# Attention, router and experts on one core: three banks for scores, four for maxima, another order within a step, and a lead-in in program order

## The chip, the core and the metric

The kernel runs on one core of one Trainium2 chip. A core has TensorE (PE, matrix products; its weight loads are shown as PEld), VectorE (DVE), ScalarE (ACT), GpSimd (POOL) and SyncE (SP), which here only issues DMAs. Matmuls write into PSUM, which has eight banks of 128 partitions x 512 float32; DVE and ACT read it. The metric is device time in microseconds (us) of one execution, lower is better. The time before is the median of three runs, 2309.47 us (2308.5 to 2316.39).

## The reference

One block of attention, a small mixing layer and a mixture of experts over x of shape 2 x 2048 x 256, all in float32:

```
qkv = x @ qkv_w + qkv_b                    # 16 heads of 16
q, k = rot(q), rot(k)                      # angles depend on the head, not on the place
attn = softmax(q @ k^T / 4)
x = layernorm(x + (attn @ v) @ out_w + out_b)
n = layer_norm(x, g1, be1)
y = x + n + (n @ mix_w + mix_b)
n = layer_norm(y, g2, be2)
probs = softmax(n @ router_w); the best 2 of 8 experts, with their weights
out = sum over the 2 of  weight * (silu(n @ w1[e] + b1[e]) @ w2[e] + b2[e])
x = layernorm(x + y + out)
```

The scores, 2 x 16 x 2048 x 2048 of them, are the bulk of the work: each is computed twice on PE, once to find the maximum of its row and once to be exponentiated.

## The kernel before

**Visits and steps.** A visit is one batch, one block of 512 queries and one group of four heads: 2 x 4 x 4 = 32 visits. A visit has 16 steps, one for each block of 128 keys, so that the attention loop has 512 steps. In a step:

- `scores(w, kt, pair)`, for two pairs of heads: two matmuls of keys by queries (L503) into two PSUM tiles, then two matmuls (L512) that add each query's negated maximum, then two exponentials on ACT (L518), each 128x512, that read those tiles. The two matmuls of a pair use different halves of PE's rows and run side by side.
- `values(w, kt, exs)`: four products of the exponentials with the values (L533), into the accumulator `av`, for the step before.
- `maxima(t, half)`, twice: two matmuls of queries by keys (L459) into two PSUM tiles, and two reductions by DVE (L467) that keep each row's maximum. They run `AHEAD` = 19 steps ahead of the scores, since a visit's maxima have to be complete before its first score.
- `work(1.0)`: small work that falls due, from a list ordered by step: transposes and projections of the next x (`prep_x`, `prep_qk`, `prep_v`), division and turning of a finished visit, the projection, the normalisations, the mixing layer, the router, and the lists of tokens per expert.

The order of PE, ACT, DVE and SP is written by hand (`manual_schedule`): each does its instructions in the program's order and waits where a semaphore is not there yet. POOL is ordered by the framework. Before, a step stands in this order: scores of both pairs, first half of the maxima, values of the step before, small work, second half of the maxima.

**Banks.** `ps_sc` has four PSUM banks for scores, `ps_mx` three for maxima and small work, `ps_av` one for the values. A pool hands its banks out in turn, so that a new tile of `ps_sc` may be written when the tile of four tiles ago has been read by ACT, and one of `ps_mx` when the tile of three tiles ago has been read. `bank(name)` gives a tile of `ps_sc` in the lead-in and of `ps_mx` afterwards; the maxima use it too.

**Lead-in.** Before the loop come the loads (x, weights, constants `cst`, tables `cs`), the rotation of the weights for q and k (L262 to L264, 24 small operations, all on DVE), the transposes of x (`prep_x`), the products for q and k (`qk_parts`) and the values. `split` in `qk_parts` divides each product into a high and a low part (L373 on DVE, L377 on DVE or POOL) and stores them four times over to memory (`stack`, L382), from where `load_stack` (L421) brings them as `km` and `qm`, the operands of maxima and scores. Then come 19 steps of maxima alone, between which `piece()` puts one matmul group of preparation after each half. Here the order was given by the framework up to the maxima.

**After the loop** the tokens, collected per expert in `x_list`, are run through the experts in 46 tiles: `turn_tile` transposes a tile's tokens (L1190, read by DVE at L1194) into a bank of its own pool `ps_t`; `hidden` and `add_tile` do the products. The last block's small work runs in between.

Of the kernel before, what the change touches and what calls it, by code (L numbers as in the profile page):

```python
# [24 lines left out]
F32 = mybir.dt.float32  # L25
# [38 lines left out]
def seq_postln_kernel(  # L64
# [86 lines left out]
    ps_mx = ctx.enter_context(tc.tile_pool(name="ps_mx", bufs=3, space=PSUM))  # L151

    with ExitStack() as actx:
# [4 lines left out]
        ps_sc = actx.enter_context(tc.tile_pool(name="ps_sc", bufs=4, space=PSUM))  # L158
# [25 lines left out]
        def load_x(b, tb):  # L184
            n = b * TPB + tb

            pool, tag, bufs = (ap_, f"km{tb % 2}", 3) if b == 0 else (ep, "x_in", 1)
            x_in[b, tb] = pool.tile([P, 4, D], F32, name=f"x_in_{n}", tag=tag, bufs=bufs)
            eng = nc.gpsimd if b == 0 and tb > 0 else nc.sync
            eng.dma_start(out=x_in[b, tb], in_=xv[n])  # L190

        with tc.tile_pool(name="wraw", bufs=1) as wp:
            wr = bp.tile([P, 2, H, 3, HD], F32, name="wr", tag="zx", bufs=1)
            cs = wp.tile([P, 2, H, 8], F32, name="cs")
            load_x(0, 0)
# [5 lines left out]
            nc.sync.dma_start(out=cst_sb, in_=cst)  # L201
            nc.scalar.dma_start(
                out=cs.rearrange("p a h d -> p (a h d)"), in_=rope.partition_broadcast(P)
            )
            for i in range(2):
                nc.gpsimd.memset(mt[i], 0.0)
            load_x(0, 1)
            load_x(0, 2)
            load_x(0, 3)
# [25 lines left out]
            dense = bp.tile([P, 4, HD], F32, name="dense", tag="comb", bufs=1)  # L235
            nc.vector.tensor_copy(dense, ident.rearrange("p (j r) -> p j r", r=32)[:, :, 0:HD])
            dense = dense.rearrange("p j d -> p (j d)")

            t3 = bp.tile([P, 2, G], F32, name="t3", tag="rest", bufs=1)
# [13 lines left out]
            for s in range(2):  # L253
                for c in range(2):
                    u1, u2 = wr[:, c, :, s, 0:8], wr[:, c, :, s, 8:16]
                    for dst, a, b_, op in (
                        (wqk[:, c, s, :, 0:8], u1, u2, ALU.subtract),
                        (wqk[:, c, s, :, 8:16], u2, u1, ALU.add),
                    ):
                        t1 = wp.tile([P, H, 8], F32, name="t1", tag="t1", bufs=2)  # L260
                        t2 = wp.tile([P, H, 8], F32, name="t2", tag="t2", bufs=2)
                        nc.vector.tensor_mul(t1, a, cs[:, 0])  # L262
                        nc.vector.tensor_mul(t2, b_, cs[:, 1])
                        nc.vector.tensor_tensor(dst, t1, t2, op)  # L264
            for c in range(2):
                nc.scalar.copy(wv[:, c], wr[:, c, :, 2, :])

            for p in range(2):
                t5 = wp.tile([P, 1], F32, name="t5", tag="t5", bufs=2)
                nc.vector.tensor_add(  # L270
                    t5, ident[:, 2 * p : 2 * p + 1], ident[:, 2 * p + 1 : 2 * p + 2]
                )
                for at in (64 + 2 * p, 65 + 2 * p):
                    nc.vector.tensor_add(t5, t5, ident[:, at : at + 1])
                nc.vector.tensor_copy(sel[p], t5.to_broadcast([P, P]))
# [17 lines left out]
        AHEAD = 19  # L293
# [37 lines left out]
        xT: dict = {}  # L331
        stack: dict = {}
# [15 lines left out]
        def qk_parts(b, tb, s, hh):  # L348


            first = leading[0]
            full, hi = (
# [18 lines left out]
            def split():  # L371

                nc.vector.tensor_single_scalar(  # L373
                    hi.bitcast(I32), full.bitcast(I32), HIGH, ALU.bitwise_and
                )
                lo = full
                (nc.vector if first and hh == 0 else nc.gpsimd).tensor_sub(lo, full, hi)  # L377
                name = f"st_{b}_{tb}_{s}_{hh}"
                t = dp.tile([8, HD, 4, 512], F32, name=name, tag=name)
                stack[b, tb, s, hh] = t  # L380
                for r, part in enumerate((hi, lo, hi, lo) if s == 0 else (hi, hi, lo, lo)):
                    (nc.sync if first else nc.gpsimd).dma_start(  # L382
                        out=t[:, :, r].rearrange("h d s -> (h d) s"), in_=part
                    )
# [33 lines left out]
        def load_stack(dst, b, tb, s, g, pair):  # L418

            at = 4 * (g % 2) + 2 * pair  # L420
            (nc.gpsimd if leading[0] else nc.sync).dma_start(  # L421
                out=dst.bitcast(F32),
                in_=stack[b, tb, s, g // 2][at : at + 2].rearrange("h d r s -> (h d r) s"),
            )

        def load_k(w):
            b, _, g = visits[w]
            km[w] = [
                ap_.tile([P, S], F32R, name=f"km_{w}_{pair}", tag=f"km{pair}", bufs=3)
                for pair in range(2)  # L430
            ]
            for tb in range(TPB):
                for pair in range(2):
                    load_stack(km[w][pair][:, tb * 512 : (tb + 1) * 512], b, tb, 1, g, pair)

        def load_q(w):
            b, qb, g = visits[w]
            qm[w] = []
            for pair in range(2):
                t = ap_.tile([P, 512], F32R, name=f"qm_{w}_{pair}", tag=f"qm{pair}", bufs=3)  # L440
                load_stack(t, b, qb, 0, g, pair)
                qm[w].append(t)

# [3 lines left out]
        def maxima(t, half):  # L447
# [8 lines left out]
            ps = [bank("ps_mx", 512) for _ in range(2)]  # L456
# [581 lines left out]
        for tb in range(TPB):  # L1038
            for c in range(2):
                prep_x(0, tb, c)  # L1040
            if tb == 0:
                dense_bias()
                prep_qk(0, 0, 0, 0)
            prep_qk(0, tb, 1, 0)
        for kt in range(0, 4, 2):
            prep_v(0, kt)
        load_q(0)
        load_k(0)
        load_q(1)
        load_k(1)  # L1050

        make_values()


        pieces: list = []
        for tb, s in [(tb, 1) for tb in range(TPB)] + [(0, 0)]:
            pieces.append(("qk", tb, s))
        for k, kt in enumerate(range(4, 16)):
            pieces.insert(1 + k + k // 2, ("v", kt))
        soon: list = []  # L1060

        def piece():

            for item in list(soon):
                item[0] -= 1
                if item[0] <= 0:
                    soon.remove(item)
                    item[1]()
            if not pieces:
                return  # L1070
            item = pieces[0]
            if item[0] == "qk":
                _, tb, s = pieces.pop(0)
                first, second, split = qk_parts(0, tb, s, 1)
                pieces.insert(0, ("fn", second, split))
                first()
            elif item[0] == "fn":
                _, second, split = pieces.pop(0)
                second()
                soon.append([2, split])  # L1080
            else:
                prep_v(0, pieces.pop(0)[1], 1)

        now[0] = 0
        at = 12
        for tb in range(1, TPB):
            small_steps(at, qk_items(0, tb, ((0, 0), (0, 1))))
            at += 4
        for tb, at in enumerate((38, 52, 104, 168)):
            later(at - 6, lambda tb=tb: load_x(1, tb))  # L1090
            small_steps(at, [(prep_x, 0.5, 1, tb, c) for c in range(2)])
            small_steps(
                at + 3,
                qk_items(1, tb, ((1, 0), (1, 1), (0, 0), (0, 1))) + v_items(1, tb),
            )
        for w in range(2, len(visits)):
            later(16 * w - AHEAD - 10, lambda w=w: load_k(w))
            later(16 * w - AHEAD - 6, lambda w=w: load_q(w))
        later(8, load_rest)
        later(36, lambda: nc.sync.dma_start(out=acc[B * S :], in_=none[:, 0:D]))  # L1100
        later(37, no_tokens)

        def max_step(t, half):
            if t < NSTEP:
                maxima(t, half)

        ET = mybir.EngineType
        with tc.manual_schedule(engines={ET.PE, ET.Activation, ET.DVE, ET.SP}):
            for t in range(AHEAD):
                now[0] = t - AHEAD  # L1110
                for half in range(2):
                    max_step(t, half)
                    piece()
                work(1.0)
            leading[0] = False
            before = None
            for t in range(NSTEP):
                now[0] = t
                w, kt = divmod(t, 16)
                exs = scores(w, kt, 0) + scores(w, kt, 1)  # L1120
                max_step(t + AHEAD, 0)
                if before is not None:
                    values(*before)
                work(1.0)
                max_step(t + AHEAD, 1)
# [8 lines left out]
    ps_t = ctx.enter_context(tc.tile_pool(name="ps_t", bufs=1, space=PSUM))  # L1134
# [49 lines left out]
    def turn_tile(t, xg):  # L1184
        ns = xg.shape[1]
        xT = wtp.tile([P, 2, ns * P], F32, name=f"xT_{t}", tag="xgT", bufs=2)
        ps = ps_t.tile([P, 2, ns * P], F32, name="ps_x", tag="t")
# [64 lines left out]
    with tc.manual_schedule(engines={ET.PE, ET.Activation, ET.DVE, ET.SP}):  # L1252
# [135 lines left out]
```

## Time and profile before

| what | value |
|---|---|
| median of three runs | 2309.47 us |
| the profiled execution's own time | 2315.68 us |
| its span in the profile | 2313.9 us |
| attention loop, from the first L503 on | from 93.1 us |
| steps of the loop that last 2.7 us, of 512 | 208 |
| L467, reductions of maxima on DVE | 2048, busy 1271.9 us, mean 682 ns |
| L518, exponentials on ACT | 2048, busy 1057.4 us, mean 604 ns |
| L459, matmuls of maxima | 2048, busy 576.0 us |
| L503 and L512, matmuls of scores | 2048 each, busy 422.6 and 419.3 us |
| L533, matmuls of values | 4096, busy 546.6 us |
| mean granted clock of TensorE | 0.985 |

The profile is one execution taken by the hardware profiler. A row of its groups names line, engine, operation, what it writes and reads, shapes and count, then busy time and the mean of one, then the engine's idle time before such instructions and what ended it. Matmuls are pipelined and their ends are modelled: the starts are recorded, and the time from one start to the next is what an instruction costs PE. The mean of an ACT or DVE instruction holds some time that overlaps the next one's start, so that busy time, a union, is less than count times mean. A weight load (PEld) goes ahead of its matmul and takes the matmul's wait: an idle time before it that ends with a reduction or an exponential may be only the time in which PE still ran earlier matmuls.

### The profile page before, as it was taken

To read this page: it belongs to the slowest core of one execution; us is meant where nothing else is said; L and a number is where in the kernel's file an instruction comes from. 1 tells how busy PE (TensorE), PEld (TensorE's weight loads), DVE (VectorE), ACT (ScalarE), POOL (GpSimd) and SP (SyncE) were. 2 spreads that over 40 slices of the span, in tenths; PEclk is the share of its full clock that TensorE was granted. 3 is DMA by queue.
4 is the path that set the end of the run, shared out by engine and by line. 5 is a ranking of instruction groups with operands and counts; after the bars stand their busy time and mean duration, and the time that the engine had idled before them with its cause. 6 is when DMAs were issued, how large, how long until landed. Compare 5 with 4: busy or idle time off the path is not lost.

```text
span 2313.9 us, 39706 instructions
## 1 busy us (share of the span) xinstructions
PE 2228.6 (96%) x14178; PEld 1337.4 (58%) x14178; DVE 1539.9 (67%) x3120; ACT 1380.4 (60%) x2722; POOL 480.4 (21%) x841
## 2 busy tenths in 40 slices
PE   6999999999999999999999999999999999999993
PEld 3445555545545555555555555555547888888882
DVE  4878778878878888888888888888815111111114
ACT  2367667766766777777777767777783222223333
POOL 3020211240123112011211201112123322222123
PEclk9799999999999999999999999999999999999996
DMA  7343321231222112112111212111046776668994
GB/s 271 114 144 119 137 101 56 74 128 62 95 99 94 46 55 74 47 66 89 66 47 56 74 49 98 56 65 56 10 132 193 207 207 192 192 187 241 305 305 155
DMA packets 173397, 275.64 MB, mean 119 GB/s; under 512 B 21648, under 2 KB 105872, under 8 KB 173200
## 3 DMA queue, kind: packets, MB, share of 16 engines
q1 hardware_dynamic: 149888, 222.95, 29.1%
q0 software_dynamic: 22896, 49.24, 7.7%
q8 instruction: 112, 1.84, 0.3%
q10 hardware_dynamic: 416, 0.92, 0.1%
q14 instruction: 85, 0.70, 0.1%
HBM read 210.31 MB, written 62.74 MB: 118 GB/s over the span
## 4 chain that ended last, share of the span: by engine, by line
PE 86%; DVE 8%; DMA 3%; issue 1%; ACT 1%; POOL 0%; SPq 0%; ACTq 0%; POOLq 0%; DVEq 0%
PE av L533 20%; PE ps_mx L459 17%; PE ps_h L1215 10%; PE ps_y L1230 10%; PE ps_sc L503 9%; PE ps_sc L512 9%; DVE pm L467 4%; PE ps_qk L361 2%; PE ps_p L594 1%; PE ps_mix L594 1%; PE ps_v L404 1%; DMA st<-full 1%; PE ps_m L491 1%; PE ps_o L555 1%; DMA b<-in_b 1%
## 5 line engine op out<-in xcount | busy, mean ns | idle before, releaser
L467 DVE TENSOR_REDUCE pm<-ps_mx 128x1 f32<-128x512 f32 x2048 | 1271.9, 682 | 201.9 <-PE ps_mx L459 197.9
L518 ACT ACTIVATE ex<-ps_sc 128x512 f32<-128x512 f32 x2048 | 1057.4, 604 | 348.9 <-PE ps_sc L512 335.9
L459 PE MATMUL ps_mx<-km,qm 64*128 64x512 f32 x2048 | 576.0, 474 | 25.9 <-DVE pm L467 17.4
L459 PEld LDWEIGHTS ps_mx<-km,qm 64*128 64x128 f32 x2048 | 289.2, 185 | 453.0 <-DVE pm L467 325.2
L533 PE MATMUL av<-ex,vt 128*32 128x512 f32 x4096 | 546.6, 605 | 0.0
L503 PE MATMUL ps_sc<-qm,km 64*128 64x512 f32 x2048 | 422.6, 395 | 0.1
L512 PE MATMUL ps_sc<-mrow,sel 64*128 64x512 f32 x2048 | 419.3, 392 | 0.0
L1222 ACT ACTIVATE hT<-ps_h,b 128x256 f32<-128x256 f32 (+1 forms) x368 | 156.2, 425 | 365.7 <-PE ps_h L1215 349.1
L1215 PE MATMUL ps_h<-xT,w 128*128 128x256 f32 (+1 forms) x1472 | 274.3, 336 | 5.1 <-ACT hT L1222 2.7
L1230 PE MATMUL ps_y<-w,hT 128*128 128x256 f32 x1136 | 255.6, 381 | 2.0 <-DVE y L1240 2.0
L1215 PEld LDWEIGHTS ps_h<-xT,w 128*128 128x128 f32 x1472 | 226.6, 190 | 48.0 <-ACT hT L1222 20.5
L1230 PEld LDWEIGHTS ps_y<-w,hT 128*128 128x128 f32 x1136 | 213.2, 191 | 29.7 <-DVE y L1240 2.4
L512 PEld LDWEIGHTS ps_sc<-mrow,sel 64*128 64x128 f32 x2048 | 204.7, 185 | 42.3
L503 PEld LDWEIGHTS ps_sc<-qm,km 64*128 64x128 f32 x2048 | 204.9, 185 | 37.9 <-ACT ex L518 14.4
L1194 DVE TENSOR_SCALAR xT<-ps_x,cols_sb 128x256 f32<-128x256 f32 (+1 forms) x92 | 40.2, 478 | 247.0 <-PE ps_x L1190 247.0
L1242 POOL DMA_INDIRECT acc<-y,xg x71 | 110.3, 1553 | 377.1 <-DVE y L1241 163.7
L533 PEld LDWEIGHTS av<-ex,vt 128*32 128x32 f32 x4096 | 81.0, 108 | 128.2 <-issue 120.5
L1240 DVE TENSOR_TENSOR y<-ps_y,b 128x256 f32<-128x256 f32 x71 | 30.1, 424 | 177.9 <-PE ps_y L1230 177.7
L132 POOL TENSOR_SCALAR op_mul<-mv 128x4 f32<-128x4 f32 x18 | 4.1, 230 | 440.7 <-DVE mv L606 439.8
L377 POOL TENSOR_TENSOR full<-full,hi 128x512 f32<-128x512 f32 x27 | 34.5, 1279 | 187.5 <-DVE hi L373 187.4
L361 PE MATMUL ps_qk<-xT,wqk 128*128 128x512 f32 x128 | 67.8, 649 | 1.1 <-ACT xT L346 1.1
L369 ACT ACTIVATE full<-ps_qk,bqk 128x512 f32<-128x512 f32 x32 | 22.0, 688 | 76.1 <-PE ps_qk L361 36.5
(201 smaller groups left out, 1149.3 us busy)
## 6 DMA issues: line engine op xcount, KB each, us to landing
w<-in_w SPq DMA_DIRECT2D x92, 1024.0 KB
km<-st SPq DMA_DIRECT2D x240, 256.0 KB
qm<-st SPq DMA_DIRECT2D x60, 256.0 KB
st<-hi POOLq DMA_DIRECT2D x44, 256.0 KB
st<-full POOLq DMA_DIRECT2D x44, 256.0 KB
xg<-x_list SPq DMA_DIRECT2D x25, 258.0 KB
b<-in_b SPq DMA_DIRECT2D x46, 128.0 KB
st<-hi SPq DMA_DIRECT2D x20, 256.0 KB
```

The source lines that it names most:

```text
L361: nc.tensor.matmul(ps, lhsT=wqk[:, c, s, 8 * hh : 8 * hh + 8, :].rearrange("p h d -> p (h d)"), rhs=xT[b, tb][:, c, :], start=(c == 0), st ...
L459: nc.tensor.matmul(ps[j], lhsT=qm[w][pair][r, qt * P : (qt + 1) * P], rhs=km[w][pair][r, kb * 512 : (kb + 1) * 512], start=True, stop=True,)
L467: nc.vector.tensor_reduce(pm[w][:, qt, 2 * pair + j, kb : kb + 1], ps[j], AX.X, ALU.max)
L503: nc.tensor.matmul(sc[j], lhsT=km[w][pair][r, kt * P : (kt + 1) * P], rhs=qm[w][pair][r, :], start=True, stop=False,)
L512: nc.tensor.matmul(sc[j], lhsT=sel[pair][r, :], rhs=mrow[w][r, :], start=False, stop=True)
L518: nc.scalar.activation(ex, sc[j], AF.Exp, scale=0.25)
L533: nc.tensor.matmul(av[32 * h : 32 * h + 32, :], lhsT=vt[b][:, kt, at : at + 32], rhs=exs[h], start=(kt == 0), stop=(kt == 15),)
L594: nc.tensor.matmul(ps[:, i, :], lhsT=turned_in[:, c, at], rhs=w[:, c, :], start=(c == 0), stop=(c == 1),)
L1215: nc.tensor.matmul(ps, lhsT=w1t[:, c, k * P : (k + 1) * P], rhs=xT[:, c, :], start=(c == 0), stop=(c == 1),)
L1222: nc.scalar.activation(hT[:, k, :], ps, AF.Silu, bias=b1[:, k : k + 1])
L1230: nc.tensor.matmul(ps, lhsT=hT[:, k, s * P : (s + 1) * P], rhs=w2t[:, k, :], start=(k == 0), stop=(k == NFC - 1),)
L1242: nc.gpsimd.indirect_dma_start(out=acc, out_offset=bass.IndirectOffsetOnAxis(ap=xg[:, s, D : D + 1].bitcast(I32), axis=0), in_=y, in_offse ...
```

## The change

It has five parts.

1. `ps_sc` gets three banks and `ps_mx` four. The maxima always take theirs from `ps_mx`, in the lead-in too.
2. A step's order becomes: scores of the first pair, values of the step before, small work, scores of the second pair, both halves of the maxima. `AHEAD` goes from 19 to 18.
3. The lead-in stands in program order on PE, ACT, DVE and SP. The constants and tables are loaded first; the other three loads of x go from POOL's queue to SP's and wait for the first operation of the rotation. The rotation for k moves to POOL, that for q stays on DVE. Four matmuls on zeros start PE. The selection columns (`make_sel`) and the copies of `wv` come later. Before the maxima begin, x of three of four blocks is prepared instead of all four; the rest goes between the halves.
4. The first products of batch 0 (`at_once`: all of k, and the first block of q, for the first eight heads) are written by DMA straight into `km` and `qm` of visit 0, 32 partitions at a time, on the queues of SP and POOL in turn; their stores to memory follow in steps 2 to 6 of the lead-in, and visit 1's loads, now on SP's queue, in step 8. Three of the six other projections of q that were small work of the first steps of the loop are done between the halves of the lead-in.
5. `ps_t` goes: `turn_tile` takes its bank from `ps_mx`.

```diff
-    ps_mx = ctx.enter_context(tc.tile_pool(name="ps_mx", bufs=3, space=PSUM))
+    ps_mx = ctx.enter_context(tc.tile_pool(name="ps_mx", bufs=4, space=PSUM))
...
-        ps_sc = actx.enter_context(tc.tile_pool(name="ps_sc", bufs=4, space=PSUM))
+        ps_sc = actx.enter_context(tc.tile_pool(name="ps_sc", bufs=3, space=PSUM))
...
-            eng = nc.gpsimd if b == 0 and tb > 0 else nc.sync
-            eng.dma_start(out=x_in[b, tb], in_=xv[n])
+            return nc.sync.dma_start(out=x_in[b, tb], in_=xv[n]).ins
...
+            rotate(nc.gpsimd, 1)
...
+            turned_ = rotate(nc.vector, 0)
+
+            for tb in range(1, TPB):
+                wait_for(load_x(0, tb), turned_[:1])
...
-        AHEAD = 19
+        AHEAD = 18
...
+            at_once = first and hh == 0 and (s == 1 or tb == 0)
...
+                for pair in range(2 if at_once else 0):
+                    to = km[0][pair][:, tb * 512 : (tb + 1) * 512] if s else qm[0][pair]
+                    to = to.bitcast(F32).rearrange("(h d r) s -> r (h d) s", d=HD, r=4)
+                    for r, part in enumerate(parts):
+                        (nc.sync, nc.gpsimd)[r % 2].dma_start(
+                            out=to[r], in_=part[32 * pair : 32 * pair + 32, :]
+                        )
...
-            ps = [bank("ps_mx", 512) for _ in range(2)]
+            ps = [ps_mx.tile([P, 512], F32, name="ps_mx", tag="mx") for _ in range(2)]
...
+            late_q = [(TPB - 2, 1), (TPB - 1, 0), (TPB - 1, 1)]
+            pieces: list = [("x", TPB - 1, c) for c in range(2)] + [("qk", TPB - 1, 1, 0)]
+            more = [("qk", tb, 1, 1) for tb in range(TPB)]
+            more += [("qk", tb, 0, hh) for tb in range(TPB) for hh in range(2) if (tb, hh) not in late_q][1:]
...
             for t in range(AHEAD):
                 now[0] = t - AHEAD
+                if t == 8:
+                    load_q(1)
+                    load_k(1)
+                elif 2 <= t < 7:
+                    stores.pop(0)()
...
-                exs = scores(w, kt, 0) + scores(w, kt, 1)
-                max_step(t + AHEAD, 0)
+                exs = scores(w, kt, 0)
                 if before is not None:
                     values(*before)
                 work(1.0)
+                exs = exs + scores(w, kt, 1)
+                max_step(t + AHEAD, 0)
                 max_step(t + AHEAD, 1)
                 before = (w, kt, exs)
...
-    ps_t = ctx.enter_context(tc.tile_pool(name="ps_t", bufs=1, space=PSUM))
...
-        ps = ps_t.tile([P, 2, ns * P], F32, name="ps_x", tag="t")
+        ps = ps_mx.tile([P, 2, ns * P], F32, name="ps_x", tag="mx")
```

## The prediction

> **What bounds the kernel now.** I read the page's busy shares and its chain of waits first, to learn which engine sets the time and in which stage.
>
> ```profile
> PE 2228.6 (96%) x14178; PEld 1337.4 (58%) x14178; DVE 1539.9 (67%) x3120; ACT 1380.4 (60%) x2722; POOL 480.4 (21%) x841
> ...
> PE 86%; DVE 8%; DMA 3%; issue 1%; ACT 1%; POOL 0%; SPq 0%; ACTq 0%; POOLq 0%; DVEq 0%
> PE av L533 20%; PE ps_mx L459 17%; PE ps_h L1215 10%; PE ps_y L1230 10%; PE ps_sc L503 9%; PE ps_sc L512 9%; DVE pm L467 4%; PE ps_qk L361 2%; PE ps_p L594 1%; PE ps_mix L594 1%; PE ps_v L404 1%; DMA st<-full 1%; PE ps_m L491 1%; PE ps_o L555 1%; DMA b<-in_b 1%
> ```
>
> The reader is to see that PE carries the chain, and that the loop of 512 steps (L459, L503, L512, L533) is 55% of it. By the starts of the L503 matmuls the loop runs from 93.1 to about 1724.5: 3.19 us a step. Next I read one step without small work, on the timeline.
>
> ```profile
> 109.89 0.49 PE L459 MATMUL ps_mx<-km,qm 64*128 64x512 f32 x2
> 110.23 0.39 PE L503 MATMUL ps_sc<-qm,km 64*128 64x512 f32 x2
> 110.42 2.48 DVE L467 TENSOR_REDUCE pm<-ps_mx 128x1 f32<-128x512 f32 x4 [0.21 <-PE ps_mx L459]
> 110.45 0.40 PE L512 MATMUL ps_sc<-mrow,sel 64*128 64x512 f32 x2
> 110.69 0.39 PE L503 MATMUL ps_sc<-qm,km 64*128 64x512 f32 x2
> 110.92 0.40 PE L512 MATMUL ps_sc<-mrow,sel 64*128 64x512 f32 x2
> 110.94 2.07 ACT L518 ACTIVATE ex<-ps_sc 128x512 f32<-128x512 f32 x4 [0.63 <-PE ps_sc L512]
> 111.15 0.52 PE L459 MATMUL ps_mx<-km,qm 64*128 64x512 f32 x2
> 111.60 1.07 PE L533 MATMUL av<-ex,vt 128*32 128x512 f32 x8
> 112.59 0.19 PEld L459 LDWEIGHTS ps_mx<-km,qm 64*128 64x128 f32 x2 [0.84 <-DVE pm L467]
> ```
>
> Ends of matmuls are modelled, so only starts are subtracted. A step is 112.59 - 109.89 = 2.70. A pair of score or maxima matmuls takes 0.23 (110.23, 110.45, 110.69, 110.92, 111.15), but 111.15 to 111.60 is 0.45: the second weight load of that pair, a single record, comes at 111.17, when the reduction that began at 110.42 has ended (111.11). That is what three maxima banks cost, about 0.2. DVE has 4 reductions at a pitch of 0.60, 2.39, ACT 4 exponentials, 2.07: both nearly full, and the four score banks keep ACT off the path, since a tile needs the exponential of four tiles ago.
>
> **The change, step by step.** A step becomes: two score tiles, values of the step before, small work, two other score tiles, four maxima. I count the tiles: with three banks the second tile of each half needs the exponential of the tile three before it. For the first half of the next step this is the first tile of the half just issued, with only the maxima in between. Is this wait the last? The last visit of before, which has no maxima, shows exactly such a wait once:
>
> ```profile
> 1696.71 0.50 PE L503 MATMUL ps_sc<-qm,km 64*128 64x512 f32 x2
> 1697.05 0.39 PE L512 MATMUL ps_sc<-mrow,sel 64*128 64x512 f32 x2
> 1697.28 0.75 PE L503 MATMUL ps_sc<-qm,km 64*128 64x512 f32 x2
> 1697.54 0.18 PEld L503 LDWEIGHTS ps_sc<-qm,km 64*128 64x128 f32 x1 [0.30 <-ACT ex L518]
> 1698.19 0.16 PEld L533 LDWEIGHTS av<-ex,vt 128*32 128x32 f32 x8 [0.36 <-issue]
> ```
>
> From it and its single records come all terms of the new cycle:
> - L512 of the second half to its exponential's start: 0.49 (110.455 to 110.943; 1697.045 to 1697.531);
> - that exponential: 0.60 (mean 0.604); its end to the weight load that it frees: 0.05 (1697.485 to 1697.536);
> - that L503 to its L512: 0.335 (1697.538 to 1697.873), 0.11 more than unstalled;
> - L512 to values: 0.32 (1697.873 to 1698.196); values' first four to last four: 0.45; values to the next L503: 0.54 (1696.166 to 1696.707);
> - that L503 to its L512: 0.34 (1696.71 to 1697.05).
>
> Sum **3.13 us, against 2.70**. The other limits: PE alone, with no wait, needs 0.45 + 0.54 + 0.34 + 0.23 + 0.23 + 0.23 + 0.23 + 0.32 = 2.57; DVE 2.39 plus 0.27 of small work (137 us of other DVE records over 512 steps) = 2.66; ACT 2.07. So the gain that four maxima banks bring is real and hidden behind the wait. Queued behind the waiting weight load on PE are the rest of that half, the values and the whole next half; ACT then waits for PE, and DVE has 0.7 free per step.
>
> Over the loop:
> - 305 steps of the first 31 visits have no small matmuls; their mean is 2.83, since some wait for DVE's small work. They become 3.13, DVE's part now covered: +0.30 x 305 = **+91**.
> - Some 175 steps carry small matmuls (four transposes add 0.59, a projection 1.93). These stand between values and the second half, on the cycle, so they add as before. +0.43, less about 0.10 of DVE waits that vanish: 0.33 x 175 = **+58**.
> - The last visit has no maxima and a mean of 2.29; the wait is the same there: (3.13 - 2.29) x 17 = **+14**. Its cover being gone costs nothing more: maxima take 0.46 of PE's idle time, no more. For the same reason 18 steps of lead instead of 19 cost nothing apart.
> - Small work puts activations into ACT's queue ahead of the second half's exponentials. A transposed copy of 0.58 that starts 0.2 after its matmuls is done before these (0.83 after the half starts); L369 with 0.69 may push them by 0.1. Between 0 and 0.3 x 170 = 50; I take **+5**, near the first end, as ACT has a third of a step free.
>
> **The lead-in** (0 to 93.1) is PE, DVE and DMA in turn. DVE's rotation waits until 10.05 for a small constant behind large loads, and the first maxima stand at 34.84, after two trips through memory: the chain has 4.21 for the store and 6.85 for the load. In the change the constants go first, loads of x come after the first rotation, POOL takes the rotation of k (12 records; 1.27 for 128x512 gives 0.3 to 0.5 for a quarter), and the split goes straight to its place: one trip, of about 4. Its 8 small DMAs stand on SP and POOL, whose queues hold nothing urgent then; the stores follow in steps 2 to 6. First maxima: weights at 6.5, rotation to 11-12, projection and activation 2.7, split 1.1, DMAs 1.8 + 4, makes 21 to 23. Then 36 half-steps at 1.49 (60.57, 62.05, 63.54): 54, ends at 76: **-16**. Bounds: -25 if nothing stalls, +3 if the 9 us stall at 46 to 55, for a buffer whose store had not landed, comes back and the DMAs are slow. Three projections of 1.93 move from the loop into half-steps that were idle: **-6**; the loop's first two steps (4.27 and 4.73) become ordinary: **-3**.
>
> Loads of x and of the next keys and queries move from POOL's queue to SP's; there SP waits for the first rotation, near 6.5, with only later DMAs of the lead-in behind it. Four warm-up matmuls, the selection columns (0.4 to 0.8 of DVE) and the copies of `wv` (0.71 of ACT) fall into idle time of the first 20 us: nothing; uncovered they would be some 2.
>
> The last stage loses its own bank for transposes and takes one of four: L1194 has 247 us of idle time before it, so nothing.
>
> Sum: 91 + 58 + 14 + 5 - 16 - 6 - 3 = **+143** on the profiled execution's own 2315.7: 2459. That execution lay 6.2 over the median of 2309.5, so I predict **2452**.
>
> **A rule against the change, weighed.** The Trainium skill, "TensorE: Matmul & The Clock Gate", section "A second HAM failure mode: psum-queue depth-cycling", says that a kernel which cycles its PSUM banks so that PE pauses briefly in each iteration can make the clock gate swing between half and full speed. The change does just this. The rows:
>
> ```profile
> 74.00:93.00 19.00, 17.82 (x37) 8.28 (x36) 18.33 (x33) 0.96 (x2) 0.86 (x2) 0.59 0.72 219
> 1686.70:1724.00 37.30, 37.30 (x268) 15.50 (x265) 5.37 (x28) 33.46 (x68) 14.08 (x37) 1.00 0.34 113
> ```
>
> The granted clock (third from the end) is 0.59 where PE only issues a 0.23 pair each 1.2, and 1.00 in the last visit, where it pauses for banks as above. The new step uses 2.57 of 3.13, 82%; nearer the second. By the rows the gate costs nothing; by the rule, at 0.59, the cycle's 1.99 of PE would be 3.37, and 480 steps would cost another 660.
>
> **Rivals.**
> 1. *The third bank's wait decides* (my forecast): 88%. For it: the same wait in the last visit. Own range 2405 to 2495: a cycle of 3.05 to 3.20 gives -38 to +34, ACT's copies up to +45, the lead-in -9 to +19; these seldom add up.
> 2. *The wait is covered and the maxima stall goes*: the step falls to PE's 2.57. That happens if the freed bank comes 0.56 earlier than in my sum, for instance if an exponential were ready before its half ended. Then 480 x -0.13 = -62, DVE waits and lead-in -35: 2212. Against it: 0.49 and 0.60 repeat in every step. 7%.
> 3. *Both cancel*: the cycle is 2.75 and the lead-in pays for it, 2309 within 0.5%. No row gives 2.75. 2%.
> 4. *The clock gate swings too*: 2452 + 660 = 3110. 3%.
>
> 0.5% of the time is what a measurement can tell from none. Faster 0.07, same 0.02, slower 0.91. The range is the first case's, a little wide: 2400 to 2497.
>
> **What would show it.** The changed profile has a group "L503 weight load" with about 0.4 us x 500 of idle time released by ACT; loop steps of 3.13, those with transposes 3.7; the pair of maxima at 0.23; DVE idle before L467 up; the last visit at 3.1 a step; the loop starting near 76. Steps under 2.8 would make the forecast wrong, and a wait on anything but ACT before L503 would make its reason wrong.

## The result, and the profile after

| | before | after |
|---|---|---|
| median of five runs on one chip | 2310.21 us | 2488.07 us (2484.64 to 2489.95) |
| ratio | | 1.0765, interval 1.0753 to 1.0778 |
| span of the profiled execution | 2313.9 us | 2486.4 us |
| mean granted clock of TensorE | 0.985 | 0.985 |

The change makes the kernel slower by 7.7%. Lines have moved: L459 is now L485 (maxima), L467 L493 (their reductions), L503 and L512 are L529 and L538 (scores), L518 L544 (exponentials), L533 L559 (values), L369 L379, L382 L402 (stores), L1190 L1239.

First the page of the changed kernel, busy shares and the chain of waits:

```profile
PE 2379.8 (96%) x14186; PEld 1296.6 (52%) x14186; DVE 1549.9 (62%) x3108; ACT 1437.2 (58%) x2724; POOL 478.6 (19%) x838
...
PE 76%; ACT 12%; issue 6%; DVE 3%; DMA 1%; POOL 1%; SPq 0%; ACTq 0%; DVEq 0%; POOLq 0%
PE av L559 19%; PE ps_sc L529 17%; ACT ex L544 10%; PE ps_h L1264 10%; PE ps_y L1279 9%; PE ps_sc L538 9%; PE ps_mx L485 2%; PE ps_qk L371 2%; PE ps_p L620 1%; PE ps_mix L620 1%; PE ps_v L429 1%; PE ps_m L517 1%; PE ps_o L581 1%; DVE pm L493 1%; PE ps_l L799 1%
```

PE still reads 96% busy, as before. The chain tells the two kernels apart: DVE goes from 8% to 3%, ACT from 1% to 12%, nearly all of it the exponentials. The maxima went from 17% to 2%, and the scores' L529 has gone from 9% to 17%.

Next one plain step of the changed kernel on the timeline, from a second half to the next second half; columns are start, time, engine, line and operation, and idle time with its releaser:

```profile
1034.40 0.50 PE L529 MATMUL ps_sc<-qm,km 64*128 64x512 f32 x2
1034.74 0.40 PE L538 MATMUL ps_sc<-mrow,sel 64*128 64x512 f32 x2
1034.97 0.62 PE L485 MATMUL ps_mx<-km,qm 64*128 64x512 f32 x4
1035.23 1.09 ACT L544 ACTIVATE ex<-ps_sc 128x512 f32<-128x512 f32 x2 [0.79 <-PE ps_sc L538]
1035.40 2.48 DVE L493 TENSOR_REDUCE pm<-ps_mx 128x1 f32<-128x512 f32 x4
1035.43 0.94 PE L529 MATMUL ps_sc<-qm,km 64*128 64x512 f32 x2
1035.88 0.18 PEld L529 LDWEIGHTS ps_sc<-qm,km 64*128 64x128 f32 x1 [0.49 <-ACT ex L544]
1035.88 0.73 PE L538 MATMUL ps_sc<-mrow,sel 64*128 64x512 f32 x2
1036.54 1.06 PE L559 MATMUL av<-ex,vt 128*32 128x512 f32 x8
1037.54 0.49 PE L529 MATMUL ps_sc<-qm,km 64*128 64x512 f32 x2
```

The step is 1037.54 - 1034.40 = 3.14 (3.13 by the single records; 3.13 is the median of the steps without small work). The four maxima are issued without a pause. Then comes the wait: of the next first half, the second weight load is held until 1035.88, when the exponential that began at 1035.23 has ended. From L538 to that weight load it is 1.14 us, in which PE issues two pairs of maxima (0.23 each) and one score matmul. Over the whole run the list of waits has

```profile
PEld ps_sc L529 <- ACT ex L544: 246.2, 502, 1.5
```

that is one wait of 0.49 in nearly each of the 512 steps. And the clock, in a stretch of such steps (PE, PEld, DVE, ACT, POOL busy, then granted clock, DMA share, GB/s):

```profile
90.00:145.00 55.00, 53.39 (x328) 22.69 (x327) 39.57 (x67) 37.13 (x68) 7.69 (x11) 1.00 0.34 108
```

The granted clock is 1.00, and it is 1.00 from 200 to 1600 us too.

**Where the 172.4 us of span come from** (by unrounded spans). By the starts of the score matmuls:

| stretch | before | after | difference | forecast |
|---|---|---|---|---|
| lead-in, to the first score | 93.1 | 89.7 | -3.4 | -16 |
| first 31 visits | 1593.6 | 1749.6 | +156.0 | +145 |
| last visit | 37.8 | 61.2 | +23.4 | +14 |
| after the loop | 589.4 | 585.9 | -3.6 | 0 |

The first 31 visits have 496 steps. Before, 321 of them had no small matmuls, at a mean of 2.83; now it is 332, at 3.14. Steps with four small matmuls, mostly transposes, went from 3.43 to 3.77 (110, now 102), those with a projection from 4.67 to 5.11 (58, now 47), and those with both from 5.38 to 5.54 (7, now 15).

The last visit has one step of 13.05 us, while most others take 3.13. Its timeline:

```profile
1870.84 0.29 PEld L1239 LDWEIGHTS ps_x<-ident,xg 128*128 128x128 f32 x2 [8.46 <-issue]
1870.87 0.66 PE L1239 MATMUL ps_x<-ident,xg 128*128 128x128 f32 x2 [8.05 <-DMA xg<-x_list]
```

L1239 is `turn_tile`, the first token tile of the last stage. Two of its transposes stand on PE inside the eighth step of the last visit, between two score matmuls, and PE waits 8.05 us there for the tokens.

In the lead-in the first maxima do start earlier, at 26.93 instead of 34.84, and the gain is then lost. Windows of the changed kernel (columns as above), and the longest wait of ACT between 42 and 92 us:

```profile
42.00:50.00 8.00, 8.00 (x28) 3.39 (x27) 7.72 (x14) 1.81 (x4) 3.03 (x4) 1.00 0.96 316
50.00:60.00 10.00, 10.00 (x38) 4.74 (x36) 8.97 (x15) 1.83 (x4) 1.35 (x2) 1.00 1.04 380
60.00:70.00 10.00, 10.00 (x34) 4.45 (x34) 9.19 (x16) 2.05 (x6) 2.54 (x2) 1.00 0.99 325
70.00:80.00 10.00, 6.11 (x16) 2.16 (x15) 4.85 (x9) 1.23 (x3) 1.26 (x1) 0.83 0.93 353
```

```profile
ACT full L379 <- DMA st<-full: 18.6, 3, 9.0
```

From 42 to 80 us the DMA engines are full (share, the number before the last, 0.93 to 1.04): the stores of 256 KB each, put off to steps 2 to 6, and visit 1's loads. ACT's copy of a product waits up to 9.0 us for a buffer whose store has not landed, and PE, whose bank that copy must empty, is busy for only 6.11 of the 10 us from 70 to 80. Before, they were that full from 20 to 50 us, and no more from 50 on. Two windows of the kernel before:

```profile
42.00:50.00 8.00, 8.00 (x27) 3.36 (x26) 7.29 (x13) 1.43 (x3) 5.19 (x9) 1.00 0.99 383
50.00:60.00 10.00, 6.09 (x16) 2.92 (x14) 4.22 (x8) 1.32 (x3) 2.35 (x2) 0.68 0.72 257
```

### The profile page after: what moved, and what is told of

Read it like the earlier page. It is cut to its first block, busy times and chain, and to the rows that moved or that the text cites. A ratio compares the mean times of both kernels' runs of the same rounds, so it can differ in the third digit from the quotient of the medians.

```text
span 2486.4 us, 39778 instructions
## 1 busy us (share of the span) xinstructions
PE 2379.8 (96%) x14186; PEld 1296.6 (52%) x14186; DVE 1549.9 (62%) x3108; ACT 1437.2 (58%) x2724; POOL 478.6 (19%) x838
## 4 chain that ended last, share of the span: by engine, by line
PE 76%; ACT 12%; issue 6%; DVE 3%; DMA 1%; POOL 1%; SPq 0%; ACTq 0%; DVEq 0%; POOLq 0%
PE av L559 19%; PE ps_sc L529 17%; ACT ex L544 10%; PE ps_h L1264 10%; PE ps_y L1279 9%; PE ps_sc L538 9%; PE ps_mx L485 2%; PE ps_qk L371 2%; PE ps_p L620 1%; PE ps_mix L620 1%; PE ps_v L429 1%; PE ps_m L517 1%; PE ps_o L581 1%; DVE pm L493 1%; PE ps_l L799 1%
## 5 line engine op out<-in xcount | busy, mean ns | idle before, releaser
L493 DVE TENSOR_REDUCE pm<-ps_mx 128x1 f32<-128x512 f32 x2048 | 1271.8, 683 | 343.5 <-PE ps_mx L485 333.5
L544 ACT ACTIVATE ex<-ps_sc 128x512 f32<-128x512 f32 x2048 | 1111.9, 594 | 444.1 <-PE ps_sc L538 424.8
L529 PE MATMUL ps_sc<-qm,km 64*128 64x512 f32 x2048 | 712.4, 472 | 40.2 <-ACT ex L544 16.8
L529 PEld LDWEIGHTS ps_sc<-qm,km 64*128 64x128 f32 x2048 | 284.3, 184 | 600.5 <-issue 339.1
L538 PE MATMUL ps_sc<-mrow,sel 64*128 64x512 f32 x2048 | 576.5, 419 | 0.2 <-ACT mrow L519 0.2
L559 PE MATMUL av<-ex,vt 128*32 128x512 f32 x4096 | 550.3, 608 | 0.0
L485 PE MATMUL ps_mx<-km,qm 64*128 64x512 f32 x2048 | 355.4, 401 | 2.1 <-DVE pm L493 2.0
L485 PEld LDWEIGHTS ps_mx<-km,qm 64*128 64x128 f32 x2048 | 221.2, 185 | 84.3 <-DVE pm L493 21.5
L538 PEld LDWEIGHTS ps_sc<-mrow,sel 64*128 64x128 f32 x2048 | 247.3, 186 | 0.5 <-ACT mrow L519 0.5
L559 PEld LDWEIGHTS av<-ex,vt 128*32 128x32 f32 x4096 | 81.1, 108 | 189.6 <-issue 177.2
L379 ACT ACTIVATE full<-ps_qk,bqk 128x512 f32<-128x512 f32 x32 | 22.0, 688 | 86.0 <-PE ps_qk L371 46.6
```

Of the source, the lines that this page charges most:

```text
L485: nc.tensor.matmul(ps[j], lhsT=qm[w][pair][r, qt * P : (qt + 1) * P], rhs=km[w][pair][r, kb * 512 : (kb + 1) * 512], start=True, stop=True,)
L493: nc.vector.tensor_reduce(pm[w][:, qt, 2 * pair + j, kb : kb + 1], ps[j], AX.X, ALU.max)
L529: nc.tensor.matmul(sc[j], lhsT=km[w][pair][r, kt * P : (kt + 1) * P], rhs=qm[w][pair][r, :], start=True, stop=False,)
L538: nc.tensor.matmul(sc[j], lhsT=sel[pair][r, :], rhs=mrow[w][r, :], start=False, stop=True)
L544: nc.scalar.activation(ex, sc[j], AF.Exp, scale=0.25)
L559: nc.tensor.matmul(av[32 * h : 32 * h + 32, :], lhsT=vt[b][:, kt, at : at + 32], rhs=exs[h], start=(kt == 0), stop=(kt == 15),)
```

## The experiments

The theory: one loop of waits, score matmul, exponential, freed bank, closes once per step and is 3.13 long; three banks and the new order make it together. The main rival: the step is bound by something else that the change added (the clock, DVE, the maxima in one block), or the loop of waits would vanish with a bank more and leave PE's 2.57.

**e1 and e2: half of the change each.** e1 keeps the three score banks and four maxima banks and has the old order; e2 keeps the new order and has the old banks (four for scores, three for maxima). e1:

```diff
-                exs = scores(w, kt, 0)
+                exs = scores(w, kt, 0) + scores(w, kt, 1)
+                max_step(t + AHEAD, 0)
                 if before is not None:
                     values(*before)
                 work(1.0)
-                exs = exs + scores(w, kt, 1)
-                max_step(t + AHEAD, 0)
                 max_step(t + AHEAD, 1)
```

e2:

```diff
-    ps_mx = ctx.enter_context(tc.tile_pool(name="ps_mx", bufs=4, space=PSUM))
+    ps_mx = ctx.enter_context(tc.tile_pool(name="ps_mx", bufs=3, space=PSUM))
...
-        ps_sc = actx.enter_context(tc.tile_pool(name="ps_sc", bufs=3, space=PSUM))
+        ps_sc = actx.enter_context(tc.tile_pool(name="ps_sc", bufs=4, space=PSUM))
```

> The changed kernel with the old order within a step (both score halves, half the maxima, values, small work, other half of the maxima), still with three banks for scores and four for maxima. Theory A (the wait for the third score bank sets the step): the second half's second tile now waits for the first half's first exponential, which nothing covers: from the first L503 0.34 to L512, 0.49 + 0.60 + 0.05 to the freed bank, 0.335 to L512, 0.23 + 0.32 to values, 0.45 + 0.54 to maxima, 0.33 to the next step: plain steps of 3.65 to 3.7, about 2750 us (2700 to 2800). Rival B (the order alone costs, since values now stand right behind a half and wait for the last exponential of the step before): back to 2.7 a step, about 2305 us.

> The changed kernel with the old banks (four for scores, three for maxima), still in the new order. Theory A: no score tile waits for ACT any more, but the fourth maximum of a step needs the bank of the first one, whose reduction ends 0.53 + 0.69 + 0.05 after its matmul: 1.27 after the first pair, where 0.23 is needed; plain steps of about 3.7, waits before L485 on DVE, about 2750 us (2650 to 2800), and the last visit, without maxima, back to 2.3 a step. Rival B (the order alone costs): as the changed kernel, 3.13 a step, 2488 us, with values (L559) waiting on ACT.

Measured: e1 2723.34 us, e2 2733.8 us, one run each (before on that chip: 2315.74). Both are slower than the whole change, as expected. The largest waits of PE for a bank, first of e1, then of e2:

```profile
PEld ps_sc L529 <- ACT ex L544: 495.0, 521, 1.8
```

```profile
PEld ps_mx L485 <- DVE pm L493: 472.9, 524, 3.0
```

In e1 the scores wait for the exponential, 0.95 us a time, twice what the change shows: all four score tiles stand in a row, so that the fourth needs the first's exponential at once. In e2 the four maxima stand in a row on three banks, so that the fourth needs the first's reduction. One part of the forecast for e2 failed: its last visit, which has no maxima, was to fall to 2.3 a step and takes 2.94. No score tile waits there; the wait is that of the values, which e6 shows below. A plain step, from the timelines:

| plain step, us | old order | new order |
|---|---|---|
| four score, three maxima banks | 2.70 | 3.62 |
| three score, four maxima banks | 3.59 | 3.13 |

Neither part has a price of its own. Each order has the number of banks that it needs, and the new pair is the worse of the two good ones.

**e3: both halves undone.** Banks and order of before; the new lead-in, the moved projections and the rest of the change stay.

```diff
-                exs = scores(w, kt, 0)
+                exs = scores(w, kt, 0) + scores(w, kt, 1)
+                max_step(t + AHEAD, 0)
...
-                exs = exs + scores(w, kt, 1)
-                max_step(t + AHEAD, 0)
...
-    ps_mx = ctx.enter_context(tc.tile_pool(name="ps_mx", bufs=4, space=PSUM))
+    ps_mx = ctx.enter_context(tc.tile_pool(name="ps_mx", bufs=3, space=PSUM))
```

> The changed kernel with the old banks and the old order within a step; lead-in, 18 steps ahead and the shared bank of the last stage as changed. Theory A: plain steps of 2.70 again; what is left is the new lead-in: 3.4 us earlier, two slow first steps and three projections gone from the loop (9 us), so 2298 us (2292 to 2306), ratio to before 0.995. A rival by which the lead-in's moved loads and stores cost later in the loop: 2310 or more.

Measured: 2312.33 us over 21 runs against 2315.74, ratio 0.9983 (0.9977 to 0.999). The plain step is 2.70 again, and the step of 13.05 is gone, so that the whole loss lies in banks and order. The 0.17% that it gains on the kernel before are less than the 0.5% from which the prediction calls a time different; the 0.5% that I expected of the lead-in are not there. By the rival they are lost later in the loop. The profile, of an execution of 2315.22 us, speaks against it: its first score stands at 97.1, 4.0 later than before, and its first 31 visits are 5.5 shorter. The lead-in is not quite that of the changed kernel, since its maxima have three banks and not four; whether that matters was not tested.

**e4: the lead-in's transfers on two queues.** e3, with half of the stores, and the second pair's loads, on POOL's queue. It tests whether SP's queue, which issues its stores one behind the other there, holds them up.

```diff
-                        (nc.sync if first else nc.gpsimd).dma_start(
+                        (nc.sync if first and r % 2 == 0 else nc.gpsimd).dma_start(
...
-            nc.sync.dma_start(
+            (nc.gpsimd if leading[0] and pair else nc.sync).dma_start(
```

> As e3, and in the lead-in every second store of a split product, and the loads of visit 1 for the second pair of heads, go on POOL's queue instead of SP's. If the lead-in's stalls (9.0 us before L379 for the landing of a store, 5.1 and 4.5 before that) come from SP's queue, which issues one DMA each 0.64 us without a pause from 42 to 69 us, the loop starts 6 to 12 us earlier: 2289 us (2284 to 2296). If they come from the time of the transfers themselves, which share the same 16 engines, nothing changes against e3.

Measured: 2312.64 us over 14 runs, ratio 0.999 (0.9981 to 0.9999): no gain over e3, against the 2289 forecast. Windows of e4, then the last two of e3:

```profile
42.00:50.00 8.00, 8.00 (x28) 3.76 (x28) 7.41 (x14) 1.81 (x4) 6.06 (x11) 1.00 0.94 310
50.00:60.00 10.00, 10.00 (x35) 4.49 (x34) 8.91 (x16) 2.05 (x5) 3.07 (x5) 1.00 1.03 357
60.00:70.00 10.00, 8.73 (x29) 3.78 (x28) 6.54 (x11) 0.70 (x3) 5.17 (x7) 1.00 0.76 242
70.00:80.00 10.00, 7.97 (x18) 3.70 (x19) 5.79 (x11) 2.65 (x6) 2.35 (x3) 0.66 0.69 269
```

```profile
60.00:70.00 10.00, 10.00 (x36) 4.91 (x36) 9.15 (x16) 2.45 (x6) 1.36 (x2) 1.00 0.98 336
70.00:80.00 10.00, 7.07 (x23) 2.88 (x21) 5.47 (x10) 1.22 (x3) 1.25 (x2) 0.98 1.02 381
```

With two queues the DMA engines are full until 60 (0.94 and 1.03), and a store on SP's queue now takes some 1.2 us to issue where it took 0.64. ACT still waits 8.9 us for a buffer whose store has not landed. From 60 on the engines are less full than in e3, and the first score stands at 92.2 instead of 97.1; but this profile is of an execution of 2309.72 us and that of e3 of one of 2315.22, each at an end of its runs, and the medians show no gain. So the single queue is not shown to be the limit. That it is the bytes is likely and not shown: a version with fewer bytes was not run.

**e5 and e6: half of the maxima left out.** If maxima, DVE or their banks bound the step, it must shrink. e5 leaves the banks at three for scores; e6 has four for scores and three for maxima, in the new order, which is free of e2's wait since there are only two maxima per step. In both, the second half of the maxima is not computed in the loop, and the first half's values stand in for it:

```diff
+            if half and not leading[0]:
+                for j in range(2):
+                    nc.vector.tensor_copy(
+                        pm[w][:, qt, 2 * pair + j, kb : kb + 1], pm[w][:, qt, j, kb : kb + 1]
+                    )
+                if i == 31:
+                    maxima_done(w)
+                return
```

> The changed kernel without the second half of each step's maxima in the loop (two matmuls and two 128x512 reductions per step are left out; two copies of one column each stand in their place). Three banks for scores, four for maxima. Theory A: the maxima stood in the time in which PE waits for the third bank, so the cycle of L512, exponential, freed bank, L503, values, L503 is as long as before: plain steps of 3.13, total within 15 us of 2488. A rival by which the step is the sum of PE's and DVE's work (a throughput limit): 0.23 or more less a step, 2375 us or less.

> As e5, with four banks for scores and three for maxima: only the number of banks differs, and the order within a step is the new one. Theory A: no score tile waits, the step falls to PE's own 0.45 + 0.54 + 0.34 + 0.23 + 0.23 + 0.23 + 0.32 = 2.34: about 2100 us (2070 to 2150). A rival by which the new order itself makes PE wait (values right behind the first half): 3.13 a step as in e5, 2488 us.

Measured: e5 2477.55 us, plain step 3.13, although two matmuls and two reductions per step are gone: neither PE's work on maxima nor DVE bounds the step. The wait for the bank takes up what the missing pair of maxima leaves, 0.73 a time instead of 0.49:

```profile
PEld ps_sc L537 <- ACT ex L552: 370.7, 511, 1.0
```

e6 2376.45 us, plain step 2.93. The wait for the third bank is gone with the fourth bank. The two versions are 101 us apart, 95 of them in the first 31 visits, but e6 stays far above the 2100 us that I expected. A line of its list of waits, and one of its steps (L567 are the values there):

```profile
PEld av L567 <- ACT ex L552: 184.7, 537, 0.7
```

```profile
1106.40 2.07 ACT L552 ACTIVATE ex<-ps_sc 128x512 f32<-128x512 f32 x4
1106.60 0.41 PE L546 MATMUL ps_sc<-mrow,sel 64*128 64x512 f32 x2
1106.94 0.24 PEld L567 LDWEIGHTS av<-ex,vt 128*32 128x32 f32 x6 [0.37 <-issue]
1107.54 0.14 PEld L567 LDWEIGHTS av<-ex,vt 128*32 128x32 f32 x2 [0.35 <-ACT ex L552]
```

The values of the step before stand right behind the first half of the next step. Their fourth product needs the second exponential of the second half: two exponentials from 1106.40 on, 0.49 and 0.59, end at 1107.49, and the weight load comes at 1107.54. That closes another loop: 0.49 from L546 to the first exponential, 0.49 + 0.59 for the two, 0.05, 0.45 + 0.52 for the rest of the values, 0.34 to the next L546: 2.93. It lies above the old kernel's 2.70.

**e11: e6 in the old order.** The same half of the maxima is left out, and the edit to the order is that of e1. There the values stand behind both halves and the maxima.

> As e6 (second half of each step's maxima left out in the loop, four banks for scores, three for maxima), but in the old order: both score halves, maxima, values, small work. In e6 plain steps took 2.93 instead of 2.34, and the fourth matmul of the values waited 0.35 for the last exponential of the step before. If it is the place of the values, right behind the next step's first half, that makes this wait, it is gone here, as a whole second half and the maxima stand between: plain steps of 2.3 to 2.4, about 2110 us (2080 to 2150). If something else holds e6 back, such as ACT or the banks, steps stay near 2.9 and the time near 2376 us.

Measured: 2119.48 us, plain steps mostly of 2.36 and 2.47. So the place of the values, not a shortage of anything in the machine, holds e6 at 2.93.

**e7 and e8: one exponential shortened.** This changes a term of the sum by itself. e7 cuts the first exponential of the second half, on the cycle by the theory, to 256 of its 512 columns, and e8 the first one of the first half, off the cycle (`pair == 0`). The other half of the tile stays at a constant. Both versions also give the temporaries of the rotation one buffer instead of two, which touches the lead-in and not the steps.

```diff
+                if pair == 1 and j == 0:
+                    ex = kept[kt % 2]
+                    nc.scalar.activation(ex[:, :256], sc[j][:, :256], AF.Exp, scale=0.25)
+                else:
+                    ex = ap_.tile([P, 512], F32, name="ex", tag="ex", bufs=8)
+                    nc.scalar.activation(ex, sc[j], AF.Exp, scale=0.25)
```

> The changed kernel with one exponential of four per step cut to half its columns: the first tile of the second half, whose bank the next step's first half waits for (the other half of the tile is left at a constant). Theory A: this one is on the cycle; it takes some 0.17 to 0.20 less, so plain steps of 2.93 to 2.96 and about 2396 us (2380 to 2410). A rival by which ACT is off the path, since it is idle for a third of the step: no change, 2488 us.

> The same cut on another exponential: the first tile of the first half. ACT has as much less work as in e7. Theory A: this one's bank is needed only by the second half of the same step, 1.1 us later, with some 0.4 to spare, so nothing changes: plain steps of 3.13, within 8 us of 2488. A rival by which ACT's total work counts: as e7.

Measured: e7 2378.95 us and 2.91 a step, e8 2465.39 us and 3.07. Two rows of e7:

```profile
982.88 0.38 ACT L548 ACTIVATE kept<-ps_sc 128x256 f32<-128x256 f32 x1 [0.85 <-PE ps_sc L541]
983.31 0.18 PEld L532 LDWEIGHTS ps_sc<-qm,km 64*128 64x128 f32 x1 [0.27 <-ACT kept L548]
```

The short exponential takes 0.384 instead of 0.598, and the step loses the 0.214, to 2.91, a little more than the forecast had it; the weight load that it frees again follows at once. The same saving off the cycle gives 0.06 and not 0.21. I had expected nothing and a time within 8 us of 2488; the 0.06 are taken up at the end.

**e9 and e10: the step of 13.05 us.** In e9 the first token tile's transposes take a bank of a pool that exists only after the loop, and so can't be moved into it. e10 is the changed kernel again, beside it on the same chip.

```diff
-        ps = ps_mx.tile([P, 2, ns * P], F32, name="ps_x", tag="mx")
+        pool, tag = (ps_mx, "mx") if t else (ps_h, "h")
+        ps = pool.tile([P, 2, ns * P], F32, name="ps_x", tag=tag)
```

> The changed kernel, but the first of the 46 transposes of token tiles takes its bank from a pool that exists only after the attention loop, so that it can't stand inside the loop. In the changed kernel two of its matmuls stand in the last visit's eighth step, where PE waits 8.05 us for the load of those tokens: that step takes 13.05 instead of 3.13. Theory: without it the step is 3.13 again, and the last stage starts some 2.5 us later after the loop: 7 us less, 2481, ratio to before 1.073. Rival: the load is needed then anyway and the last stage waits for it instead: no change against the changed kernel.

> The changed kernel once more, on the same chip as e9, for the comparison: ratio to before 1.0765 as measured.

Measured: e9 2481.21 us, ratio 1.0722 (1.0703 to 1.074); e10 2489.05 us, ratio 1.0761 (1.0743 to 1.0779). The eighth step of the last visit takes 3.13 in e9, and the kernel is 7.8 us faster: the 9.9 us of the stall, less some 3 that the last stage loses by starting its first tile later (589.0 after the loop in e9's profile, 585.9 in that of the change).

Sharing the pool is not enough for the stall. In e2, e3, e4, e6 and e11 the last stage shares it too, but the pool has three banks; there the first of these transposes starts behind the loop's last score matmul (e3: 1725.42 behind 1722.32). In every version with four banks except e9 it stands in the eighth step, which takes 12.69 to 14.02. So the stall needs both the shared pool and its fourth bank. Which wait the fourth bank removes was not looked into.

## Why the prediction was right, and where it missed

**The mechanism is the one forecast.** The wait is before the scores' second weight load, released by ACT, at about 0.49 in 502 cases (forecast: 0.4 in 500). The plain step is 3.13 to 3.14 (forecast: 3.13), each of its eight terms comes back within 0.01 in the single records of the step shown, and e7 shows that a change of one term moves the step by just that. The maxima's own stall is gone and worth nothing, as argued: their pairs now follow each other without pause, and e5 shows that even with half of them left out the step is no shorter. The total of 2488 lies near the upper end of the forecast's own range, 2405 to 2495.

**Rival 2, the step at PE's 2.57,** supposes the wait gone. It was wrong by more than its chance says: where a fourth bank does take the wait away, with half of the maxima away as well, the step in this order stops at 2.93, as it does in e2's last visit. My list of limits (PE, DVE, ACT, the bank) lacked the values' wait for the last exponential. It did no harm to the forecast because 2.93 is below 3.13; I had not worked that out, so this was luck.

**Rival 4, the clock gate.** The row shows 1.00 with one pause of about half a microsecond per step, as the row of the last visit had suggested. The Trainium skill ("TensorE: Matmul & The Clock Gate", "A second HAM failure mode: psum-queue depth-cycling") tells of one bf16 kernel whose clock swung between half and full speed when its PSUM banks were cycled in each iteration; the loop of this float32 kernel does not do so, and the measurement decides. **Rival 3** found no step near 2.75.

**Where the 36 us between 2452 and 2488 come from.** By the table of stretches the span's sum of +143 fell short by 29.4, in four terms:

- *The lead-in's -16* measured -3.4, the largest miss (12.6; from 93.1 to 76 it is 17, too, and not 16). The first maxima came 7.9 earlier, not 12 to 14, and then the stores that I let "follow in steps 2 to 6" filled the DMA engines until 80. The prediction's bound of +3 named the stall that came back, 9.0 us for a buffer whose store had not landed, but its middle left it out. The sum had priced the stores' place in the queue, where nothing urgent stood, and not their bytes. That the bytes are the cause is argued from the windows, and not shown. A single profile fixes this term only to a few us: in e10, the same kernel, the first score stands at 88.2 instead of 89.7.
- *First 31 visits,* +156.0 against +145. The plain steps' +0.31 was right, but not their number: the sum has 305 + 175 = 480 steps, and there are 496. The trace before has 321 plain steps, and 16 x 0.30 is 5 of the 11. The two slow first steps are among these 321 and in their mean of 2.83, so that the -3 for them counts them twice. Steps with small work are each 0.05 above the sum (3.77 against 3.13 + 0.59, 5.11 against 3.13 + 1.93), over 149 steps 7, where the sum had set down 5. The three together make the 11, roughly.
- *The last stage's shared bank, "nothing",* cost 7.8 (e9). I had looked at the idle time before the transposes, so at the time when the bank is wanted, and not at what else the shared pool allows: with its own pool gone, two transposes could be placed ahead of scores of the last visit, where PE takes them in order and waits 8.05 for their tokens. The stall of 9.9 accounts for the last visit's 9.4 over the forecast. Without it the visit would be 13.5 longer, close to the +14, though the sum takes 17 steps at 2.29 and the trace before has 16 at 2.36. That the pool also had four banks was the other half of it.
- *After the loop* -3.6 against 0, since the last stage has its first tile partly done (in e9, where it has not, 589.0 are left of 589.4).

Another 6.2 are the correction from the profiled execution to the median: the one before lay 6.2 above its median, the one after at its own, so that there was nothing to take off. The rest is rounding.

## What to carry to other kernels

When banks move from one stage to another, write down for each tile which read has to be over before it may be written (tile n waits for the reader of tile n - bufs), add up the loop of waits that this closes, from measured starts, and do so for every operand that comes back from another engine: in this kernel, with the new order, the bank's loop was 3.13, the values' loop behind it 2.93, and PE's own work 2.57. Banks and order have to be chosen together, since either half of this change alone cost more than both. Sharing a pool with a later stage can also let that stage's instructions move up into the loop, as here with four banks and not with three: look in the profile for the later stage's lines among the loop's. Transfers that are put off still have to fit between the others, so count their bytes against the DMA engines' time as well as their places in a queue; that the bytes decided here is likely, not shown.

## What was not expected of the hardware

In e8 an exponential that is not the shortened one starts sooner: 0.43 us after its L541 (1024.519 to 1024.946) instead of 0.49. Its rows:

```profile
1024.52 0.40 PE L541 MATMUL ps_sc<-mrow,sel 64*128 64x512 f32 x2
1024.95 1.08 ACT L551 ACTIVATE ex<-ps_sc 128x512 f32<-128x512 f32 x2 [0.95 <-PE ps_sc L541]
```

In the changed kernel the same exponential waits on two semaphores, PE's and one of its own engine, and a separate semaphore record of 0.017 stands ahead of it; in e8 it carries its one wait itself. The traces show it throughout: of the exponentials that find ACT idle, 382 in e8 have no such record ahead of them and start 0.43 after their matmul (median), while 469 in the kernel before have one and start after 0.49. That this second wait is the 0.06, and so the gain of e8, fits these traces; a version that drops only this wait was not run.
